# Start-up products, order of sums and the last pairs in a four-layer modulated 1-D convolution kernel

## The chip, the core and the metric

The kernel runs on one core of one Trainium2 chip. The metric is device time in microseconds (us) for one execution, as the median of several runs; the kernel before takes 500.55 us (three runs, 499.84 to 500.64). One more execution was recorded by the profiler. All times inside the kernel are counted from the start of that execution's span.

The engines are TensorE (PE; its weight loads are shown as PEld), VectorE (DVE), ScalarE (ACT), GpSimd (POOL) and SyncE (SP, which issues nearly all DMAs here). SBUF is the working memory, PSUM the memory that PE writes its products to. Each engine runs its own instructions in the order of the program and waits on semaphores for the others. All data are fp32; on PE a product of fp32 operands shows as two passes in the trace, each with its own weight load, so counts of PE rows are twice the number of products in the code.

## The reference

128 samples, each with 64 channels and 1024 positions, go through four convolution layers whose weights are modulated by a style vector per sample, and the input is added at the end:

```python
def _layer(x, style, w, b, mw, mb, typ):
    s = style @ mw.T + mb
    weight = SCALE * w * s[:, None, :, None]
    demod = lax.rsqrt(jnp.sum(weight * weight, axis=(2, 3)) + EPS)
    weight = weight * demod[:, :, None, None]
    if typ == 'same':
        out = jax.vmap(_conv_same)(x, weight) + b[None, :, None]
    elif typ == 'upsample':
        out = jax.vmap(_conv_up)(x, weight.transpose(0, 2, 1, 3)) + b[None, :, None]
        out = _blur(out, 2.0 * blur_k, (1, 1))
    elif typ == 'downsample':
        xb = _blur(x, blur_k, (2, 2))
        out = jax.vmap(_conv_down)(xb, weight) + b[None, :, None]
    return out

out = x
for i, typ in enumerate(('same', 'upsample', 'same', 'downsample')):
    out = _layer(out, style, weights[i], biases[i], mod_w[i], mod_b[i], typ)
return x + out
```

Each layer has 64 input and 64 output channels and three taps. There is no nonlinearity between the layers, so for one sample the whole network, its two blurs included, is one linear filter with nine taps, apart from a few positions at both ends.

## The kernel before

The kernel uses that. For every sample it multiplies the four layers' weights into one nine-tap filter and applies this filter to the sample's input. Samples are held in 64 pairs (two samples fill the 128 partitions); one iteration q of the main loop (L1040, 32 iterations) handles pairs p = 2q and p + 1, and prepares filters and inputs of later ones.

**The filter chain.** For four samples at a time: `scale3` scales the last layer's weights by the table `tA` into `wd`; `stage1` (products L346 into `psS`) joins them with layer 2 and copies the result, scaled by `tB`, to `S`; `stage2` (products L377 into `psR`) joins `S` with layer 1 and the blurs, which are held ready in the nine tiles of `E`, and copies to `R`, scaled by `tC`; `stage3` (products L414 into `psW`, two parts) joins `R` with layer 0 into the filter `Wf`. `combine` (L446, DVE) makes from `Wf` the further filters `H` that a fast form of the convolution needs, with fewer products and more additions.

**The convolution of one pair.** `pre1(p)` makes sums `G` of shifted inputs on DVE (L483, L488), issues the load of a third of a later pair's input, and lets POOL make two of the five rows of `T` (L494, L495). `pre2(p)` makes the other three on DVE (L506, L516) and issues the load of the other two thirds. PE computes three products: `convA12` and, later, `convA3` write `psA`; ACT copies the first of them, negated, to `m` (L561). Then DVE forms the sums: `seed1` makes `u`, `v` and `y`, and `seed2` writes two sums into the PSUM tile `Y`, into which the products of `convB` are then accumulated. (All of these are L567.) [...] `output` (L613 on ACT, L615 on DVE) scales the result and adds the constant, `store` writes it out (L618). `Y` is one tile for nearly all pairs, so `seed2` of the next pair waits until `output` of this one has read it. In the last iterations separate PSUM tiles take its place (`Y2`).

**The order.** The program sets the order by hand; there is no scheduler (`manual_schedule`). `seed` is `seed1` and `seed2`. Ahead of the loop stand the parameter loads, the first products with the style (L189), the sums of squares (`q2_sum`, `var_matmul`, L210), the square root on ACT (`var_root`, L221), reciprocals and Newton steps on DVE, the tables on POOL and DVE, and the filters of the first samples. `blur_scale` (L286) makes four scaled copies `w1s` of layer 1's weights on ACT; `blur_matmul` (L290) sums them, tap by tap, with the identity as the other factor, into two banks of `Y`; `blur_copy` (L309) copies both to `E`. Tables and constants come for 16, then 16, then the remaining 96 samples (`PART`); those of the later parts are spread over the first iterations (`SLOTS`, `EXTRA`). The end positions of all samples are computed by a small side path, for which POOL clears some tiles (`zeros`, L719, 13 memsets; their first reader comes in q=9).

In an iteration the part that matters here is

```python
        convA12(p + 2)
        if q:
            if q < NQ - 2:
                pre2(p + 3)
            store(p, 0)
            if q == 1:
                seed2(p + 1)
            pre1(p + 4)
            store(p, 1)
            if q > 1:
                seed(p + 1)
```

after which come the second part of `stage3`, `convA3(p + 2)` and `convB(p + 1)`, whose accumulation needs `seed2(p + 1)`. SP takes loads and stores in this same order, each waiting for its data.

Of the kernel before, what the change touches and what calls it, by code (L numbers as in the profile page):

```python
# [48 lines left out]
F32 = mybir.dt.float32  # L49
# [5 lines left out]
C = 64  # L55
K = 3
# [7 lines left out]
def kernel(  # L64
# [13 lines left out]
    NQ = B // 4  # L78
# [55 lines left out]

# [3 lines left out]
    nc_v.memset(Z, 0.0)  # L138
# [147 lines left out]
    def blur_scale():  # L286
        for i in range(K + 1):
            nc_a.activation(w1s[:, i], w1r, AF.Copy, scale=BLUR2[i])

    def blur_matmul(ps):  # L290

        for b in range(len(BLUR2)):
            w = w1s[:, min(b, len(BLUR2) - 1 - b)]
            for r, rows in enumerate(HALF):

                both = b % 2 == r
                src = w[rows, 0::2] if both else w[rows, 1]
                at = (b if both else b + 1) // 2
                for cols in HALF:
                    nc.tensor.matmul(  # L300
                        ps[r][cols, C * at : C * (at + 1 + both)],
                        idn[rows],
                        src,
                        start=(b == 0),
                        stop=(b == len(BLUR2) - 1),
                        skip_group_check=True,
                    )
# [58 lines left out]
    def stage2(q, pool=None, engs=(nc_a, nc_a), between=None):  # L366
        st = chain[q]
        ps = unit(pool or ps_w, f"psR{q}")
        for n, e in enumerate((-2, -1, 0, 1, 2, 3, 4, 5, 6)):
            if e % 2 == 0:  # L370
                a, lo, m = slice(0, 5, 2), e // 2 + 1, 3
            else:
                a, lo, m = slice(1, 4, 2), (e + 3) // 2, 2
            for r, rows in enumerate(HALF):
                for c, cols in enumerate(HALF):
                    src = st[c if r == 0 else 1 - c]
                    nc.tensor.matmul(  # L377
                        ps[r][cols, lo * C : (lo + m) * C],
                        E[rows, e // 2 + 1 + (e % 2) * 5, :],
                        src[rows, a, :],  # L380
                        start=(n == 0),
                        stop=(n == 8),
                        skip_group_check=True,
                    )
# [133 lines left out]
    def pre2(p):  # L518
        pre2a(p)
        pre2b(p)  # L520
# [70 lines left out]
    def seed(p):  # L591
        seed1(p)
        seed2(p)

# [280 lines left out]
    L2, L01, L3 = slice(2, 3), slice(0, 2), slice(3, 4)  # L875
    zeros_to_y(2, 512)
# [4 lines left out]
    blur_scale()  # L881
# [8 lines left out]
    var_root(PART[0], pm[0][1], L2)  # L890
    nc_a.activation(wsq[T, L3], wio[T, L3], AF.Square)
# [4 lines left out]
    scale3(0, BOTH)  # L896
    q2_sum(L01)
    blur_copy(psB, BOTH)
# [55 lines left out]
    convA3(1)  # L954
    pre1(2)
    pre2(2)
    const_rest(2, PART[0], const_of(2, PART[0]))
    var_root(PART[1], var_of(PART[1]))
    combine(1)
    seed1(1)  # L960
# [79 lines left out]
    for q in range(NQ):  # L1040
        p = 2 * q
        c, s = q + 2, q + 3
        if q == 1:
            nc.sync.dma_start(Xe, x_ends)
            zeros()
# [19 lines left out]
        convA12(p + 2)  # L1065

        if q:
# [3 lines left out]
            if q == 1:  # L1071
                seed2(p + 1)
            pre1(p + 4)
            store(p, 1)
            if q > 1:
                seed(p + 1)
            if q == NQ - 2:
                pre2(p + 3)
        else:
# [3 lines left out]
            pre2(p + 3)  # L1083
# [3 lines left out]
            for of in (table_C, vector_c0, table_3, vector_Da):  # L1087
                of(PART[1])
            pre1(p + 4)
# [4 lines left out]
        if q == NQ - 2:  # L1094
            convA12(p + 3)
            convA3(p + 3)
        side = SLOTS.get(q)
        convB(p + 1, (lambda: slot(*side)) if side else None)
        if q == NQ - 2:
            seed(p + 2)  # L1100

            Y2[p + 3] = unit(ps_conv, "Y3")
            zeros_to_y(2, 2 * NB, p + 3)
            seed(p + 3)
        output(p + 1, 0)
        output(p + 1, 1, nc_a if q < NQ - 2 else nc_v)
        if c == NQ - 1:
# [94 lines left out]
```

## Time and profile before

| | |
|---|---|
| median of three runs | 500.55 us (499.84 to 500.64) |
| profiled execution | 501.63 us, of which span 499.8 us |
| mean granted PE clock over the span | 0.998 |
| busy: PE / DVE / ACT / POOL | 487.3 / 443.5 / 323.0 / 135.2 us |
| instructions: PE / DVE / ACT / POOL | 12620 / 937 / 787 / 195 |
| `psA` products (convA), 64x170 | 4608 passes, 304 ns each, 208.8 us busy |
| `Y` products (convB), 64x170 | 3072 passes, 304 ns each, 141.9 us busy |
| HBM read / written | 35.46 / 33.62 MB |

Passes on PE overlap (the 64x64 tiles of the array work side by side), so the mean length of one pass is several times the spacing at which they follow one another; spacing is read from the timeline, as the time of a group over its count. DVE's instructions overlap a little too: one begins up to 0.1 us before the last one's end. A time after an instruction in a timeline row, in brackets, is the idle time before it and what ended it.

In the profiled execution the loop begins at about 33 us (products of `stage2(2)`), and from about 120 us on one iteration takes 14.4 us.

### The profile page before, as it was taken

The numbers are of one execution on the slowest core, as the hardware profiler recorded it, in microseconds if no ns is written. First come the engines' busy times: TensorE is split into PE (matmuls) and PEld (weight loads), VectorE is DVE, ScalarE is ACT, GpSimd is POOL, SyncE is SP. The second block draws the span as 40 slices with busy tenths as digits, with TensorE's granted clock in tenths as the row PEclk, the third lists the DMA queues.
The fourth block names the chain that finished last, engine by engine and source line by source line (L and its number), as shares of the span: only waits on it lengthen the run. The fifth ranks groups of instructions, "written<-read, shape, count | busy, mean of one in ns | idle before, by whom it ended". The sixth has DMA issues, their size and how long they took to land.

```text
span 499.8 us, 28326 instructions
## 1 busy us (share of the span) xinstructions
PE 487.3 (97%) x12620; PEld 476.7 (95%) x12620; DVE 443.5 (89%) x937; ACT 323.0 (65%) x787; POOL 135.2 (27%) x195
## 2 busy tenths in 40 slices
PE   7999899999999999999999999999999999999994
PEld 5899889999999999999999999999999999999994
DVE  4989999999999979987979998869999989888895
ACT  3546666677676667666667666667667667766653
POOL 2234533344222222222122122212222212221210
PEclk9999999999999999999999999999999999999999
DMA  8124554454454444443544454444444446443123
GB/s 260 45 90 139 169 155 138 145 169 139 132 163 147 141 144 146 142 155 126 149 145 148 134 157 146 145 134 145 143 145 148 152 128 186 142 148 130 65 109 127
DMA packets 37449, 70.90 MB, mean 142 GB/s; under 512 B 4176, under 2 KB 28752, under 8 KB 37328
## 3 DMA queue, kind: packets, MB, share of 16 engines
q1 hardware_dynamic: 37248, 68.85, 43.8%
q8 instruction: 99, 1.62, 1.4%
q10 hardware_dynamic: 80, 0.25, 0.1%
q14 instruction: 22, 0.18, 0.1%
HBM read 35.46 MB, written 33.62 MB: 138 GB/s over the span
## 4 chain that ended last, share of the span: by engine, by line
PE 84%; DVE 11%; DMA 2%; issue 1%; ACT 1%; SPq 0%; DVEq 0%; ACTq 0%
PE psA L534 28%; PE Y L534 20%; PE psR L377 15%; PE psW L414 12%; PE psS L346 6%; PE psE L763 2%; DVE Y L567 2%; DVE T L516 1%; DVE G L483 1%; DMA par_oi<-in_params_oi 1%; DVE u L567 1%; DVE v L567 1%; DVE G L488 1%; DMA out<-o 1%; DVE T L506 1%
## 5 line engine op out<-in xcount | busy, mean ns | idle before, releaser
L534 PE MATMUL psA<-T,H 64*64 64x170 f32 x4608 | 208.8, 304 | 0.3 <-ACT R L324 0.3
L534 PEld LDWEIGHTS psA<-T,H 64*64 64x64 f32 x4608 | 191.8, 133 | 1.2 <-ACT R L324 0.5
L534 PE MATMUL Y<-T,Wf 64*64 64x170 f32 x3072 | 141.9, 304 | 3.1 <-DVE Y L567 3.1
L494 POOL TENSOR_TENSOR T<-G 128x342 f32<-128x342 f32 x62 | 58.0, 935 | 315.7 <-DVE G L488 187.3
L534 PEld LDWEIGHTS Y<-T,Wf 64*64 64x64 f32 x3072 | 129.5, 133 | 4.7 <-ACT m L561 3.4
L613 ACT ACTIVATE o<-Y,oc,dm 128x340 f32<-128x340 f32 (+1 forms) x126 | 80.0, 635 | 56.1 <-PE Y L534 54.5
L414 PE MATMUL psW<-R,par_oi 64*64 64x256 f32 (+3 forms) x1536 | 101.0, 349 | 0.0
L567 DVE SCALAR_TENSOR_TENSOR Y<-psA,u 128x340 f32<-128x340 f32 (+1 forms) x134 | 66.7, 502 | 36.8 <-ACT o L613 34.1
L377 PE MATMUL psR<-S,E 64*64 64x192 f32 (+1 forms) x2304 | 94.4, 299 | 0.1
L324 ACT ACTIVATE Wf<-psW,t 128x256 f32<-128x256 f32 (+1 forms) x252 | 75.5, 382 | 23.0 <-PE psW L414 22.9
L414 PEld LDWEIGHTS psW<-R,par_oi 64*64 64x64 f32 x1536 | 87.1, 133 | 2.7
L377 PEld LDWEIGHTS psR<-S,E 64*64 64x64 f32 x2304 | 87.4, 133 | 0.3 <-ACT S L324 0.2
L324 ACT ACTIVATE R<-psR,tC 128x448 f32<-128x448 f32 x63 | 36.6, 631 | 54.9 <-PE psR L377 54.9
L613 ACT ACTIVATE o<-y,oc,dm 128x170 f32<-128x170 f32 x125 | 65.7, 526 | 0.0
L495 POOL TENSOR_TENSOR T<-G 128x342 f32<-128x342 f32 x62 | 59.4, 957 | 0.0
L516 DVE TENSOR_TENSOR T<-G 128x684 f32<-128x684 f32 x64 | 57.8, 903 | 0.0
L483 DVE SCALAR_TENSOR_TENSOR G<-X 128x688 f32<-128x688 f32 x64 | 56.3, 879 | 0.0
L346 PE MATMUL psS<-wd,par_oi 64*64 64x192 f32 x768 | 46.2, 329 | 0.0
L346 PEld LDWEIGHTS psS<-wd,par_oi 64*64 64x64 f32 x768 | 38.6, 136 | 0.5 <-ACT raw L631 0.3
L561 ACT ACTIVATE m<-psA 128x340 f32<-128x340 f32 x64 | 29.2, 456 | 12.8 <-PE psA L534 5.3
L567 DVE SCALAR_TENSOR_TENSOR y<-psA,v 128x340 f32<-128x340 f32 x64 | 32.7, 511 | 2.2
L488 DVE SCALAR_TENSOR_TENSOR G<-X 128x342 f32<-128x342 f32 x64 | 33.4, 521 | 0.0
(132 smaller groups left out, 385.2 us busy)
## 6 DMA issues: line engine op xcount, KB each, us to landing
out<-o SPq DMA_DIRECT2D x126, 255.0 KB, 2.9
X<-in_x SPq DMA_DIRECT2D x60, 344.0 KB, 3.1
X<-in_x SPq DMA_DIRECT2D x60, 172.0 KB, 3.2
X<-in_x SPq DMA_DIRECT2D x4, 516.0 KB, 6.7
Xe<-in_x_ends SPq DMA_DIRECT2D x1, 512.0 KB, 4.9
par_oi<-in_params_oi SPq DMA_DIRECT2D x2, 208.0 KB, 5.1
out<-o SPq DMA_DIRECT2D x2, 170.0 KB, 3.3
par_io<-in_params_io ACTq DMA_DIRECT2D x1, 240.0 KB, 4.1
```

The source lines that it names most:

```text
L324: nc_a.activation(dst, src, AF.Copy, scale=f)
L346: nc.tensor.matmul(ps[r][cols, k * C : (k + K) * C], woi[rows, 2, k, :], src[rows, :], start=(k == 0), stop=(k == K - 1), skip_group_check ...
L377: nc.tensor.matmul(ps[r][cols, lo * C : (lo + m) * C], E[rows, e // 2 + 1 + (e % 2) * 5, :], src[rows, a, :], start=(n == 0), stop=(n == 8 ...
L414: nc.tensor.matmul(ps[r][cols, (lo - t_lo) * C : (hi - t_lo) * C], woi[rows, 0, k, :], rt[c][rows, lo - k : hi - k, :], start=(k == order[0]),
L483: nc_v.scalar_tensor_tensor(g[:, PL:], X[:, : 2 * PL], 0.5, X[:, PL:], op0=ALU.mult, op1=ALU.subtract)
L488: nc_v.scalar_tensor_tensor(plane(g, 2), plane(X, 3), 0.5, plane(X, 2), op0=ALU.mult, op1=ALU.subtract)
L494: eng.tensor_add(t[:, 2, :NJ], plane(g, 2), plane(g, 1))
L495: eng.tensor_sub(t[:, 3, :NJ], plane(g, 2), plane(g, 1))
L516: nc_v.tensor_sub(t[:, 0:2, :NJ], both(a, PL), both(b, 1))
L534: nc.tensor.matmul(ps[s][cols], w, Ts[p][rows, SLOT[m], j : j + NB], start=(g == 0 and m not in (0, 4)), stop=(g == 2), skip_group_check=True,
L567: nc_v.scalar_tensor_tensor(out, x, f, y, op0=ALU.mult, op1=ALU.add)
L613: nc_a.activation(dst, src, AF.Identity, bias=add, scale=d3)
```

## The change

Six things are changed.

1. `Z` is cleared in two halves, and `zeros_to_y(2, 256)` is put ahead of the first `zeros_to_y(2, 512)`, `zeros_to_y(2, 192)` ahead of `blur_matmul`.
2. `blur_scale` runs in two parts, with the square root of layer 2 (`var_root`) between them.
3. `blur_matmul` takes each tap offset with all its taps that fall into a bank in one product: bank 0 holds tiles 0 to 4 of `E`, bank 1 tiles 5 to 8, now in rising order of the tap (so `stage2` finds them at another index). 28 products of 64 or 128 columns (56 passes) become 18 of 64 to 192 (36 passes). `blur_copy` has both copies on ACT, ahead of `q2_sum(L01)`.
4. Ahead of the loop `seed1(1)` and `combine(1)` come before `pre2(2)`; in iteration 0 `pre2(3)` comes after the tables of the second part. In iterations 1 and 2 the sums of pair p + 1 come before `pre2(p + 3)` and `pre1(p + 4)`.
5. `zeros()` moves from iteration 1 to iteration 5.
6. In iteration 30 `convA3` of the last pair comes after `convB` of pair 61 and the first half of its output, the second half of the output comes ahead of the last pair's sums, and `seed_last` writes these into PSUM before it makes `v` and `y`.

On DVE this gives, in q=1: `Y` of pair 3, then `pre2(5)`, `pre1(6)`, `pre2(6)`, `pre1(7)`; in q=2: the sums of pair 5, then `pre2(7)`, `pre1(8)`, `pre2(8)`, `pre1(9)`. The order on SP's queue stays, and so does the number of instructions on DVE and POOL but for the second memset of `Z` and the copy that goes to ACT.

```diff
@@ -131,11 +131,11 @@
     one = const.tile([P, 1], F32, name="one")
     eps = const.tile([P, 1], F32, name="eps")
     Z = const.tile([P, 512], F32, name="Z")
-
     E = const.tile([P, NT, C], F32, name="E")
     w1s = const.tile([P, K + 1, K, C], F32, name="w1s")
     nc_v.memset(one, 1.0)
-    nc_v.memset(Z, 0.0)
+    nc_v.memset(Z[:, :256], 0.0)
+    nc_v.memset(Z[:, 256:], 0.0)
     nc_v.memset(eps, EPS)
 
     nc_a.activation(one, one, AF.Sqrt)
@@ -283,26 +283,32 @@
         table(nc_g, t3, bs, ALT, ODD, dm[:, 3, bs], var[:, 3, bs])
 
 
-    def blur_scale():
-        for i in range(K + 1):
+    def blur_scale(ks):
+        for i in ks:
             nc_a.activation(w1s[:, i], w1r, AF.Copy, scale=BLUR2[i])
 
     def blur_matmul(ps):
 
-        for b in range(len(BLUR2)):
-            w = w1s[:, min(b, len(BLUR2) - 1 - b)]
+
+        n = len(BLUR2)
+        plan = [[], []]
+        for b in range(n):
+            for r, (lo, hi) in enumerate(((0, 5), (5, NT))):
+                i, j = max(lo, b), min(hi, b + K)
+                if i < j:
+                    plan[r].append((b, i, j, lo))
+        for k in range(max(map(len, plan))):
             for r, rows in enumerate(HALF):
-
-                both = b % 2 == r
-                src = w[rows, 0::2] if both else w[rows, 1]
-                at = (b if both else b + 1) // 2
+                if k >= len(plan[r]):
+                    continue
+                b, i, j, lo = plan[r][k]
                 for cols in HALF:
                     nc.tensor.matmul(
-                        ps[r][cols, C * at : C * (at + 1 + both)],
+                        ps[r][cols, C * (i - lo) : C * (j - lo)],
                         idn[rows],
-                        src,
-                        start=(b == 0),
-                        stop=(b == len(BLUR2) - 1),
+                        w1s[rows, min(b, n - 1 - b), i - b : j - b],
+                        start=(k == 0),
+                        stop=(k == len(plan[r]) - 1),
                         skip_group_check=True,
                     )
 
@@ -376,7 +382,7 @@
                     src = st[c if r == 0 else 1 - c]
                     nc.tensor.matmul(
                         ps[r][cols, lo * C : (lo + m) * C],
-                        E[rows, e // 2 + 1 + (e % 2) * 5, :],
+                        E[rows, e + 2, :],
                         src[rows, a, :],
                         start=(n == 0),
                         stop=(n == 8),
@@ -592,6 +598,17 @@
         seed1(p)
         seed2(p)
 
+    def seed_last(p):
+
+        m1, m2, m3 = part.pop(p)
+        u, v = m_tile("u", p), m_tile("v", p)
+        y1s[p] = mpool.tile([P, 2, NB], F32, tag="y1", name=f"y1_{p}", bufs=3)
+        sum_of(u, m2, -1.0 / 3.0, m1)
+        part[p] = m3, u
+        seed2(p)
+        sum_of(v, m2, 1.0 / 3.0, m1)
+        sum_of(y1s[p], m3, 2.0 / 6.0, v)
+
     os = {}
 
     def convB(p, between=None):
@@ -873,12 +890,13 @@
     LATER = slice(PART[0].stop, B)
     n_later = NL * (B - PART[0].stop)
     L2, L01, L3 = slice(2, 3), slice(0, 2), slice(3, 4)
+    zeros_to_y(2, 256)
     zeros_to_y(2, 512)
     nc_v.tensor_scalar_mul(mbs, mb, SCALE)
     mod_matmul(PART[0], pm[0][0])
 
     nc_a.activation(wsq[T, L2], wio[T, L2], AF.Square)
-    blur_scale()
+    blur_scale((0, 1))
     zeros_to_y(2, 256)
     mod_scale(PART[0], pm[0][0])
     mod_square(PART[0])
@@ -888,14 +906,16 @@
     var_matmul(PART[0], pm[0][1], (2,))
     nc_v.tensor_mul(wsq[T, L01], wio[T, L01], wio[T, L01])
     var_root(PART[0], pm[0][1], L2)
+    blur_scale((2, 3))
+    zeros_to_y(2, 192)
     nc_a.activation(wsq[T, L3], wio[T, L3], AF.Square)
     psB = [Y[:, r] for r in range(2)]
     blur_matmul(psB)
     first_inverse(PART[0])
     table_A(PART[0], d2)
     scale3(0, BOTH)
+    blur_copy(psB, (nc_a, nc_a))
     q2_sum(L01)
-    blur_copy(psB, BOTH)
     q2_sum(L3)
     table_0(PART[0])
     table_02(PART[0])
@@ -952,12 +972,13 @@
     const_first(2, PART[0])
     var_matmul(PART[1], var_of(PART[1]), start=False)
     convA3(1)
+
     pre1(2)
-    pre2(2)
     const_rest(2, PART[0], const_of(2, PART[0]))
     var_root(PART[1], var_of(PART[1]))
+    seed1(1)
     combine(1)
-    seed1(1)
+    pre2(2)
     pre1(3)
 
 
@@ -1042,6 +1063,7 @@
         c, s = q + 2, q + 3
         if q == 1:
             nc.sync.dma_start(Xe, x_ends)
+        if q == 5:
             zeros()
         if c < NQ:
             stage2(c)
@@ -1063,16 +1085,16 @@
                         store(p + 1, r, slice(0, NB) if i == 0 else slice(NB, HO))
             break
         convA12(p + 2)
-
         if q:
+            if q < 3:
+
+                (seed2 if q == 1 else seed)(p + 1)
             if q < NQ - 2:
                 pre2(p + 3)
             store(p, 0)
-            if q == 1:
-                seed2(p + 1)
             pre1(p + 4)
             store(p, 1)
-            if q > 1:
+            if q > 2:
                 seed(p + 1)
             if q == NQ - 2:
                 pre2(p + 3)
@@ -1080,12 +1102,12 @@
             store(p, 0)
             store(p, 1)
             seed2(p + 1)
-            pre2(p + 3)
             var_inverse(PART[1])
             var_newton(PART[1])
             table_A(PART[1], dm[:, 2, PART[1]])
             for of in (table_C, vector_c0, table_3, vector_Da):
                 of(PART[1])
+            pre2(p + 3)
             pre1(p + 4)
         EXTRA.get((q, 0), lambda: None)()
         if c < NQ:
@@ -1093,17 +1115,18 @@
         convA3(p + 2)
         if q == NQ - 2:
             convA12(p + 3)
-            convA3(p + 3)
         side = SLOTS.get(q)
         convB(p + 1, (lambda: slot(*side)) if side else None)
+        output(p + 1, 0)
         if q == NQ - 2:
             seed(p + 2)
+            convA3(p + 3)
 
             Y2[p + 3] = unit(ps_conv, "Y3")
             zeros_to_y(2, 2 * NB, p + 3)
-            seed(p + 3)
-        output(p + 1, 0)
         output(p + 1, 1, nc_a if q < NQ - 2 else nc_v)
+        if q == NQ - 2:
+            seed_last(p + 3)
         if c == NQ - 1:
 
             banks = unit(ps_w, "Y2")
```

## The prediction

> **What bounds the kernel now.** I read the page first: TensorE (PE) is busy 97% of the span and holds 84% of the chain that ended last, so in the long middle only less PE work or fewer PE gaps could help, and the change takes no PE work out of the middle.
>
> ```profile
> PE 487.3 (97%) x12620; PEld 476.7 (95%) x12620; DVE 443.5 (89%) x937; ACT 323.0 (65%) x787; POOL 135.2 (27%) x195
> ...
> PE 84%; DVE 11%; DMA 2%; issue 1%; ACT 1%; SPq 0%; DVEq 0%; ACTq 0%
> ```
>
> Next the waits of the whole trace: PE stood still three times for the sums that VectorE (DVE) writes into `Y`. The timeline places them at convB(3) (58.82, after 1.47), convB(5) (75.23, after 1.34) and convB(11) (119.81, after 0.27).
>
> ```profile
> PE Y L534 <- DVE Y L567: 3.1, 3, 1.5
> ```
>
> Then the waits of DVE alone from 28 to 121 us: two for ACT's read of `Y` (0.40 at 79.64, 0.98 at 88.90) and one at 28.41 for `m`. Otherwise its instructions touch.
>
> ```profile
> DVE Y L567 <- ACT o L613: 1.4, 2, 1.0
> DVE u L567 <- ACT m L561: 0.9, 1, 0.9
> ```
>
> The stretches say the same: DVE is full from 41 to 75 and nearly so to 120, and eases only later (12.41 of 14.40).
>
> ```profile
> core 0: us, PE busy (x) PEld busy (x) DVE busy (x) ACT busy (x) POOL busy (x), PEclk, DMA share, GB/s
> 57.00:75.00 18.00, 15.42 (x398) 14.62 (x390) 17.72 (x35) 11.06 (x29) 10.19 (x21) 1.00 0.67 201
> 105.00:120.00 15.00, 14.73 (x393) 14.30 (x389) 14.70 (x31) 10.57 (x27) 6.73 (x11) 1.00 0.52 147
> 300.00:314.40 14.40, 14.40 (x392) 14.40 (x388) 12.41 (x26) 9.89 (x24) 3.59 (x4) 1.00 0.50 148
> ```
>
> So: from about 28 to 120 DVE sets the pace, afterwards PE. Last the start, PE only:
>
> ```profile
> 1.48 1.98 PE L170 MATMUL Y<-Z 64*64 64x512 f32 x8 [1.48 <-DVE eps L139]
> 4.89 1.13 PE L170 MATMUL Y<-Z 64*64 64x256 f32 x8
> 6.82 0.69 PE L300 MATMUL Y<-w1s,par_oi 64*64 64x128 f32 x4 [0.48 <-ACT w1s L288]
> 7.81 2.29 PE L300 MATMUL Y<-w1s,par_oi 64*64 64x64 f32 x50 [0.30 <-DMA par_oi<-in_params_oi]
> ...
> 10.00 2.13 PE L346 MATMUL psS<-wd,par_oi 64*64 64x192 f32 x22
> ```
>
> and the tile `psS` in the first 25 us, where the same 64x192 product takes 524 ns early and 322 late:
>
> ```profile
> L346 PE MATMUL psS<-wd,par_oi x72: 322/323/524, 9.8 to 21.0; 64*64 64x192 f32 x72
> ```
>
> PE runs at about half pace at first: 24 passes of `psS` cost 2.1 us at 10.0 and 0.97 at 60.9. Weight loads fall from 228 ns to 133 at 13.1 us, though the clock column prints 1.00 throughout. The fast pace came 5.3 us after the last gap of PE (0.30 before 7.81); earlier gaps are 0.46 at 3.46 and 0.48 at 6.34.
>
> **The change, part by part. (1) Start.** The halved memset of `Z` (0.48) lets PE begin 0.24 sooner, at about 1.25. One more fill of 256 columns (8 passes, 1.13 measured for such a group, some 0.9 where groups overlap) closes the gap up to 3.92; it may push the `par_s` products by up to 0.3, which `q` (ready 5.88) mostly hides. The fill of 192 columns (about 0.7) closes 6.34 to 6.82. The first four blur passes then last until the second `par_oi` half lands (7.76). PE has no gap left from 1.25 on, unless the 16-column products (3.92 to 4.96) count as one. If 5.3 us without a gap are enough, PE is fast by 1.25 + 5.3 = 6.6; if the count starts behind the 16-column products, by 10.2; if the fills count for nothing, at about 13 as before.
> The square root L221 moves ahead of two of the four `w1s` scalings (0.28 each): 6.86 to about 6.4, so `wd` is ready at 8.5 in place of 8.98. That hides under the blur products and is worth nothing while they end later.
> Blur: 56 passes become 36 with the same 5376 columns. Only four (768 columns) can precede 7.81. The remaining 4608 columns cost, at the slow 0.45 ns per column (2.1 us / 24 / 192), about 2.05: end 9.85, against 10.1. At the fast 0.21 (0.97 us) they cost 0.97, or 1.12 at 35 ns per pass (72 `psR` passes in 2.50): end 8.95. `blur_copy` moves its second half (0.42) from DVE to ACT, which idles 1.35 there; DVE had waited for ACT's half anyway, so no cost.
> Stage 1 follows (2.1 slow, 0.97 fast), then ACT's `S` (before: 12.04). `R` (15.77) needs `tC`, which DVE and POOL finished at 15.52, 3.5 after `S`. So `R` comes at `S` + 3.5 where PE is fast. Fast by 6.6: `S` 10.05, `R` 13.6, gain 2.15. Fast by 10.2: `S` 11.1, `R` 14.6, gain 1.2. Slow: gain 0.35. From `R` to `u` at 28.41 the same chain follows, and DVE has 0.94 of waiting there, so the gain is carried whole. I take 2.15, because the 5.3 is an upper bound on what PE needed; 0.35 stays in the range.
> [...]
>
> **(2) Before and in iteration 0.** `pre2(2)` leaves its place behind `pre1(2)`. Before, its L516 cost 1.58 in place of 0.86, since POOL added `T` then; L700 behind it cost 0.69. Now DVE reaches `var` early, but `var` waits for ACT's `nw`, which stands behind `m` (33.48 to 33.93) and ends 34.3. `seed1(1)` and `combine(1)` queue behind that wait. Line by line (`u`, `v`, `y` 1.38, `combine` 2.85, `pre2` 1.21, `pre1` 1.20) the sums of pair 1 end at 42.05 against 41.77, just before convB(1) at 42.19. Then `pre2(3)`, moved behind the PART[1] tables, escapes its own collision (1.58), and `u` of pair 2 comes at 46.6 against 46.67: zero, bounds -0.1 to +0.45. The loads issued with `pre2` and `pre1` move with them, and stores behind them on SP by at most one seed (2.4); their data is used some 29 us later.
>
> **(3) Iterations 1 and 2: sums first.** In q=1 `Y` of pair 3 begins at 55.7 rather than 57.62 and ends 56.7, before PE arrives (57.08): convB(3) gains 1.7. In q=2 the whole seed (2.36) goes ahead of `pre2(7)` and `pre1(8)`, and convB(5) loses its wait too. But DVE does no less work. And POOL's two `T` additions, released by `pre1`, used to run beside sums from PSUM; now they run beside `pre2` and the next `pre1`. What that costs stands in q=1 of before, DVE first, POOL second:
>
> ```profile
> 60.22 0.87 DVE L516 TENSOR_TENSOR T<-G 128x684 f32<-128x684 f32 x1
> 61.00 1.59 DVE L483 SCALAR_TENSOR_TENSOR G<-X 128x688 f32<-128x688 f32 x1
> 62.51 1.22 DVE L488 SCALAR_TENSOR_TENSOR G<-X 128x342 f32<-128x342 f32 x1
> ```
> ```profile
> 60.31 1.55 POOL L494 TENSOR_TENSOR T<-G 128x342 f32<-128x342 f32 x1
> 61.81 1.54 POOL L495 TENSOR_TENSOR T<-G 128x342 f32<-128x342 f32 x1
> ```
>
> They take turns: 59.79 to 63.65 took 3.86, the same four at 84.04 to 86.45 took 2.41. For q=2 that puts 3.86 where 2.78 stood (74.99 to 77.77): +1.1. POOL's `T` of pair 9 slides behind the POOL tables (2.76) into `combine(4)`: one more collision of 0.73 is likely (0 to 1.2). Against it DVE loses its two waits, 0.40 and 0.98. Sum at `Y` of pair 7: 1.1 - 0.40 + 0.73 - 0.98 = +0.45, so convB(7) is released 0.45 later than before and PE's gain of q=1 and 2 is given back there. From there DVE's instructions touch up to convB(11) (119.81), so 0.45 stays; bounds -0.7 and +1.5.
> [...]
>
> **(4) Rest.** `zeros()` (13 memsets, 58.40 to 60.37) goes to q=5, where POOL idles from 114.0 to 117.4 and DVE's operations beside memsets kept their length: 0 (if DVE did feel it, 0.3). In the last iterations PE's work is only reordered; before, PE was short of work by 0.17 once (seeds of pair 63, 491.6). Now `m` of pair 63 waits for convA3(63) and ACT's output, about 490.1; `u` and `Y` take 1.5 and end 491.65, PE arrives 491.75: -0.1, bounds -0.3 and +0.4. The tail of outputs and stores after 493.6 stays.
>
> **Sum:** -2.15 + 0 + 0.45 + 0 - 0.1 = -1.8. The profiled execution took 501.63 with a span of 499.8, 1.83 lying around it; it would become 499.83, span 498.0. The runs' median is 1.08 below that execution, so 500.55 - 1.8 = 498.75.
>
> **Rivals.** *Start stays slow or turns late*: fills of zeros or 16-column products may not bring the fast pace forward. For: the fill before 3.46 brought none. Against: gaps followed it. Gain 0.35 to 1.2, net 0 to -0.85: about 500.1.
> *DVE's debt decides (slower)*: from 28 to 120 DVE has 1.38 of waits to give; if `combine(4)` meets both additions (1.2) and q=0 costs 0.45, the sum is +1.4, and with a start of 0.35 the time is 501.6. It decides once the loop loses 1.0 more than the start gains. For: DVE full at 119.81. Against: the start.
> *Both waits are won*: PE keeps 1.75 + 1.62. Against: convB(11) waited already, and its release can come sooner only by DVE's 1.38. With a fast start and no collision: 500.55 - 2.15 - 1.38 = 497.0.
>
> **How the numbers follow.** Forecast 0.46, slow or late start 0.27, DVE's debt 0.19, waits won 0.08. Within 0.2% (1.0 us) is what this kernel's runs cannot tell from no change. Nine tenths of the forecast are faster (0.41), a fifth of the second (0.05), all of the last (0.08): 0.54. Slower: 0.17 of the third. The rest, 0.29, is the same. Range 497.5 to 501.3: it cuts half of either end case. The forecast's own range is 498.0 to 499.7.
>
> **What would show it.** Right: weight loads near 133 ns in the blur or in stage 1, `S` at about 10 to 11, `u` of pair 0 at 26.2; no wait at convB(3) and convB(5), but one of about 1 at convB(4) or convB(7); L483 or L516 near 1.6 in q=2; PE without gaps from 120 less 1.7. Wrong: `S` after 11.5; DVE waiting in q=3 to 5, which would mean more slack than I count; a wait at convB(63).

## The result and the profile after

The changed kernel takes 500.55 us as the median of 14 runs (499.13 to 501.15); the kernel before, run beside it, takes 500.51 (14 runs, 499.64 to 501.08). The ratio is 0.9998 with a 95% interval of 0.9989 to 1.0007: no difference that can be measured. The time lies in the stated range (497.5 to 501.3), but the forecast of 498.75 did not come. Of the cases named, the first rival (about 500.1) lies nearest, though not for its reason alone.

The profiled execution of after took 501.05 us with a span of 499.24. Before's took 501.63 (span 499.85), which is above every one of its 14 runs. So the two traces differ by 0.6 where the medians do not differ at all. Of that, 0.50 lies behind the last scaling of an output, in the last stores: this tail took 4.21 in before, 3.71 in after, and 3.64 to 4.11 in the eight traces below, with either order of the end. What the change does is therefore read at landmarks inside the trace:

| us from the span's start | before | after | after less before |
|---|---|---|---|
| `S` of the first samples | 12.04 | 11.54 | -0.50 |
| `R` | 15.77 | 15.03 | -0.74 |
| `u` of pair 0 | 28.41 | 27.73 | -0.68 |
| `stage2` (its first weight load) in iterations 2 and 3 | 64.20, 81.16 | 61.78, 77.84 | -2.42, -3.32 |
| `stage2` in iteration 4 | 95.68 | 94.58 | -1.10 |
| `stage2` in iteration 29 (about the same from 6 on) | 465.89 | 465.12 | -0.77 |
| last product of PE | 493.57 | 493.46 | -0.11 |

The start gained 0.7, the early loop gained 2.6 more and gave all of it back, and the last iterations lost 0.65. The page shows the same shares as before, busy times and chain:

```profile
PE 487.2 (98%) x12616; PEld 474.9 (95%) x12616; DVE 444.0 (89%) x937; ACT 322.5 (65%) x788; POOL 133.7 (27%) x195
...
PE 85%; DVE 11%; issue 1%; ACT 1%; DMA 1%; SPq 0%; DVEq 0%
```

The waits of the whole trace, after (who waits, for whom; total, times, longest). PE's waits for the sums in `Y` had been 3.1 us in three pieces:

```profile
PE Y L540 <- DVE Y L573: 2.8, 3, 1.7
```

Still three, and nearly as much. The timeline of PE says which (start, duration, and in brackets the idle time before):

```profile
65.25 1.96 PE L540 MATMUL Y<-T,Wf 64*64 64x170 f32 x48 [0.53 <-DVE Y L573]
...
89.30 1.10 PE L540 MATMUL Y<-T,Wf 64*64 64x170 f32 x24 [1.72 <-DVE Y L573]
```

```profile
491.50 1.96 PE L540 MATMUL Y<-T,Wf 64*64 64x170 f32 x48 [0.52 <-DVE Y L573]
```

The waits at convB(3) and convB(5) (1.47 and 1.34 before) are gone. In their place stand convB(4) at 65.25, convB(7) at 89.30 and, in the last iterations, convB(63) at 491.50. The waits of DVE between 24 and 121 us show what it had to give and gave, its two waits for ACT's read of `Y` (1.4):

```profile
DVE u L573 <- ACT m L567: 0.9, 1, 0.9
DVE var L222 <- ACT nw L221: 0.6, 1, 0.6
```

And the stretches, where DVE is as full as before and PE's gap has only moved, from 57 to 75 (15.42 busy before, 17.26 now) into 75 to 90:

```profile
core 0: us, PE busy (x) PEld busy (x) DVE busy (x) ACT busy (x) POOL busy (x), PEclk, DMA share, GB/s
...
57.00:75.00 18.00, 17.26 (x453) 15.99 (x450) 17.76 (x34) 10.86 (x28) 4.70 (x6) 1.00 0.56 172
75.00:90.00 15.00, 13.28 (x348) 12.52 (x344) 14.79 (x29) 9.95 (x25) 8.61 (x13) 1.00 0.60 182
```

**The start.** PE's timeline of after:

```profile
1.22 2.84 PE L170 MATMUL Y<-Z 64*64 64x256 f32 x16 [1.22 <-DVE Z L137]
3.98 0.81 PE L189 MATMUL psM<-par_s 128*64 128x16 f32 x16
4.72 0.66 PE L170 MATMUL Y<-Z 64*64 64x256 f32 x8
5.78 0.23 PE L210 MATMUL psM<-ssq,q 64*64 64x16 f32 x2 [0.39 <-DVE q L205]
...
7.57 2.04 PE L306 MATMUL Y<-w1s,par_oi 64*64 64x64 f32 x32 [0.49 <-DMA par_oi<-in_params_oi]
9.33 2.11 PE L352 MATMUL psS<-wd,par_oi 64*64 64x192 f32 x24
```

The rows `Y<-Z` are the fills: products with the zero tile `Z` that `zeros_to_y` issues into `Y`. The eight passes at 4.72 take 0.66 where the same group took 1.13 in before: PE does turn fast early, sooner than the 6.6 us I forecast. But a fill that takes 0.66 in place of 1.13 ends sooner, and what it was to cover comes open again, 0.39 ahead of 5.78 and 0.49 ahead of 7.57. And the blur (32 passes in 2.04) and `stage1` (24 passes in 2.11, the slow figure of before) run at the slow pace again. Stretches of after, with the granted clock in the third column from the right:

```profile
core 0: us, PE busy (x) PEld busy (x) DVE busy (x) ACT busy (x) POOL busy (x), PEclk, DMA share, GB/s
...
4.40:7.80 3.40, 2.42 (x44) 1.29 (x46) 2.49 (x13) 1.96 (x8) 0.80 (x4) 1.00 1.02 281
7.80:11.20 3.40, 3.40 (x56) 3.24 (x49) 1.41 (x5) 1.14 (x3) 2.73 (x10) 0.50 1.02 410
11.20:13.10 1.90, 1.52 (x43) 1.39 (x41) 1.31 (x4) 1.56 (x5) 0.00 (x0) 1.00 0.28 98
```

The clock falls to 0.50 from 7.80 to 11.20, behind 3.40 us in which PE was busy for only 2.42. Blur and `stage1`, which were to gain, fall into just this stretch.

This is one execution. The clock averaged over the span is on record for all 14 runs (0.993 to 1.000), and a stretch of 3.4 at 0.50 would take 0.003 off it, so the ten runs at 0.998 and above held no such stretch. Their median is 500.54 (499.13 to 500.96). The slow stretch alone therefore cannot be why the forecast did not come. How early the pace turned in those runs is not known, since the average does not show the slow pace ahead of the first turn (before's column prints 1.00 there too).

**The turns of DVE and POOL** fall where the prediction had them. After, q=2, DVE first, POOL second:

```profile
75.29 1.59 DVE L489 SCALAR_TENSOR_TENSOR G<-X 128x688 f32<-128x688 f32 x1
76.81 1.22 DVE L494 SCALAR_TENSOR_TENSOR G<-X 128x342 f32<-128x342 f32 x1
...
80.30 1.12 DVE L458 SCALAR_TENSOR_TENSOR H<-Wf 128x384 f32<-128x384 f32 x1
```

```profile
74.67 1.48 POOL L500 TENSOR_TENSOR T<-G 128x342 f32<-128x342 f32 x1 [9.92 <-PE Y L540]
76.10 1.55 POOL L501 TENSOR_TENSOR T<-G 128x342 f32<-128x342 f32 x1
...
80.07 0.94 POOL L501 TENSOR_TENSOR T<-G 128x342 f32<-128x342 f32 x1
```

L489 takes 1.59 (0.87 alone) and L494 1.22 (0.50 alone) beside POOL's two additions, and the first operation of `combine(4)` 1.12 (0.55 alone) beside the addition at 80.07. That they take turns by whole instructions is seen in the ends: POOL 76.15, DVE 76.88, POOL 77.65, DVE 78.03. Each ends 0.73 to 0.77 behind the other engine's end, the shorter L494 0.38 behind it.

### The profile page after: what moved, and what is told of

Same layout as the page of the kernel before. It is cut to its first block, busy times and chain, and to the rows that moved or that the text cites. A ratio compares the mean times of both kernels' runs of the same rounds, so it can differ in the third digit from the quotient of the medians.

```text
span 499.2 us, 28320 instructions
## 1 busy us (share of the span) xinstructions
PE 487.2 (98%) x12616; PEld 474.9 (95%) x12616; DVE 444.0 (89%) x937; ACT 322.5 (65%) x788; POOL 133.7 (27%) x195
## 4 chain that ended last, share of the span: by engine, by line
PE 85%; DVE 11%; issue 1%; ACT 1%; DMA 1%; SPq 0%; DVEq 0%
PE psA L540 29%; PE Y L540 19%; PE psR L383 15%; PE psW L420 13%; PE psS L352 6%; PE psE L780 2%; DVE T L522 2%; DVE G L489 2%; DVE Y L573 2%; DMA par_oi<-in_params_oi 1%; DVE G L494 1%; DVE u L573 1%; DVE T L512 1%; DVE v L573 1%; DVE H L458 0%
## 5 line engine op out<-in xcount | busy, mean ns | idle before, releaser
L500 POOL TENSOR_TENSOR T<-G 128x342 f32<-128x342 f32 x62 | 57.6, 929 | 318.5 <-DVE G L494 189.7
L501 POOL TENSOR_TENSOR T<-G 128x342 f32<-128x342 f32 x62 | 58.6, 946 | 0.0
L522 DVE TENSOR_TENSOR T<-G 128x684 f32<-128x684 f32 x64 | 57.0, 890 | 0.0
L489 DVE SCALAR_TENSOR_TENSOR G<-X 128x688 f32<-128x688 f32 x64 | 56.9, 889 | 0.0
L494 DVE SCALAR_TENSOR_TENSOR G<-X 128x342 f32<-128x342 f32 x64 | 33.2, 519 | 0.0
```

What stands on the lines that cost most here:

```text
L489: nc_v.scalar_tensor_tensor(g[:, PL:], X[:, : 2 * PL], 0.5, X[:, PL:], op0=ALU.mult, op1=ALU.subtract)
L494: nc_v.scalar_tensor_tensor(plane(g, 2), plane(X, 3), 0.5, plane(X, 2), op0=ALU.mult, op1=ALU.subtract)
L500: eng.tensor_add(t[:, 2, :NJ], plane(g, 2), plane(g, 1))
L501: eng.tensor_sub(t[:, 3, :NJ], plane(g, 2), plane(g, 1))
L522: nc_v.tensor_sub(t[:, 0:2, :NJ], both(a, PL), both(b, 1))
```

## The experiments

Three runs take the change apart, three test a cause each, one changes the writes at the end, and one puts the answers together. The theory of the start that they test is a guess from after's clock, which stood at 0.50 for 3.4 us behind 3.40 us with only 2.42 busy: that the pace is set in stretches of this length, which may begin elsewhere in another execution, that a busy stretch brings the fast pace and that one with gaps brings the slow pace back. The theory of the loop is DVE's debt and its turns with POOL (1.59 for 0.87 above). A ratio is taken over all runs and is not quite that of the two medians. "Net" below is always the time between two landmarks of a trace, so that a run's own start or tail does not enter. Of each trace, `u` of pair 0 to `stage2` of iteration 6 is called the loop (96.67 us in before, 96.60 in after), and `stage2` of iteration 29 to PE's last product the end (27.68 and 28.34).

**The start alone** (items 1 to 3 of the change in the kernel before).

```diff
-    nc_v.memset(Z, 0.0)
+    nc_v.memset(Z[:, :256], 0.0)
+    nc_v.memset(Z[:, 256:], 0.0)
...
+    zeros_to_y(2, 256)
     zeros_to_y(2, 512)
...
-    blur_scale()
+    blur_scale((0, 1))
...
     var_root(PART[0], pm[0][1], L2)
+    blur_scale((2, 3))
+    zeros_to_y(2, 192)
```

> Only the start-up edits (fills, halved clear of Z, square root sooner, larger blur products, both copies on ACT) on the kernel before. Theory A (PE's pace is granted by stretches of time of which a busy one releases the slow pace and one with gaps brings it back): the first sums of pair 0 (u, 28.41 before, 27.73 after the whole change) come anywhere from 25.8 to 28.4 according to the run, with slow weight loads (near 228 ns) somewhere between 6 and 12 us in most of them; the median stays within 0.15% of before. Theory B (the fast pace is owed a fixed time after the first product, so the start gains a fixed amount): u at 27.7 again, and a median 0.7 us (0.14%) lower. Both: waits at convB(3) and convB(5) of about 1.5 us as before, since the loop's order is as before.

Measured: 500.89 against 501.46, ratio 0.9992 (0.9983 to 1.0002). Here PE's timeline shows another start than after's, with the same code:

```profile
4.34 1.04 PE L190 MATMUL psM<-par_s 128*64 128x16 f32 x16 [0.28 <-DMA par_s<-in_params_s]
5.31 1.13 PE L171 MATMUL Y<-Z 64*64 64x256 f32 x8
...
7.26 2.46 PE L307 MATMUL Y<-w1s,par_oi 64*64 64x192 f32 x36
9.53 1.17 PE L353 MATMUL psS<-wd,par_oi 64*64 64x192 f32 x24
```

The fill at 5.31 is slow (1.13), the blur too, and only `stage1` is fast (1.17). `S` comes at 10.81, `R` at 14.29 and `u` at 26.94, 1.47 ahead of before: the "fast by 10.2" case of the prediction. The same start code gives `u` between 27.60 and 27.87 in after and in four runs below. Before's own start varies as much: `u` at 28.41, 27.39 and 28.69 in the three traces that have it. The means are 27.60 (six traces) and 28.16 (three), so the start is worth some 0.6 by the traces, and 0.57 by the medians of this run. Neither is clear of the spread: starts of the same code lie 0.9 to 1.3 apart, and the interval of the ratio takes in 1.

**The loop alone** (items 4 and 5).

```diff
+        if q == 5:
             zeros()
...
+            if q < 3:
+                (seed2 if q == 1 else seed)(p + 1)
             if q < NQ - 2:
                 pre2(p + 3)
...
-            if q > 1:
+            if q > 2:
                 seed(p + 1)
```

> Only the order of sums ahead of and in iterations 0 to 2, and the later clearing, on the kernel before. Theory DVE's debt (DVE sets the pace to about 120 us; waits of PE are moved, not removed): from u of pair 0 to convB(11) 91.3 to 91.5 us as in both kernels (91.40 before, 91.32 after); no wait at convB(3) and convB(5), about 0.5 at convB(4) and 1.7 at convB(7); median within 0.1% of before. Theory PE's waits (each wait that is removed is time won): 88.0 to 88.5 us from u to convB(11), median 3 us (0.6%) lower.

Measured: 501.30, ratio 0.9993 (0.9983 to 1.0002); the loop 96.54, so -0.13 net. `stage2` comes 2.46 and 3.12 earlier in iterations 2 and 3 (this trace's start is 1.02 early), 1.53 earlier in iteration 4, and PE waits 1.36 at convB(7). The gain of the two waits is won and given back with no help from the start or the end. In iterations 23 to 27 this trace loses another 0.5 against before, in two steps that after does not show; their cause was not found.

**The end alone** (item 6).

```diff
             convA12(p + 3)
-            convA3(p + 3)
...
+        output(p + 1, 0)
         if q == NQ - 2:
             seed(p + 2)
+            convA3(p + 3)
...
-            seed(p + 3)
-        output(p + 1, 0)
         output(p + 1, 1, nc_a if q < NQ - 2 else nc_v)
+        if q == NQ - 2:
+            seed_last(p + 3)
```

> Only the reordered last pairs on the kernel before. Theory late seeds: the four writes of the last pair's sums into Y follow one another at 0.38 us and take 1.48, so convB(63) waits 0.5 us where it waited 0.15, and PE ends 0.4 to 0.65 us later relative to convB(11) (373.8 from convB(11) to PE's end before, 374.4 after); the stores after PE's end are done 0.5 sooner (4.2 us from the last scaling to the end before, 3.7 after); sum 0.0 to 0.2 us. Rival (the last stores were what the edit was for, and they carry the end): span 0.5 us shorter from convB(11) to the end.

Measured: 501.94, ratio 1.0008 (0.9999 to 1.0016). The loop is before's to the hundredth (96.67) and the end takes 28.35, 0.67 more, with the same wait of 0.52 at convB(63). So the end's order costs what after loses there. The tail behind the last scaling took 3.95, not the 0.5 less than before's 4.21 that was expected; before's order itself gave 3.80, 4.11 and 3.64 in other traces, so the tail does not hang on this order.

**More fill ahead of the blur** (in after; the fills only hold PE busy).

```diff
     blur_scale((0, 1))
-    zeros_to_y(2, 256)
+    zeros_to_y(2, 512)
...
     blur_scale((2, 3))
-    zeros_to_y(2, 192)
+    zeros_to_y(2, 512)
+    zeros_to_y(2, 512)
```

> The changed kernel with fills that keep PE busy at the fast pace as well: 512 columns in place of 256 behind the style products, twice 512 in place of 192 ahead of the blur. Theory A (gaps bring the slow pace back): weight loads of the blur and of stage 1 near 133 ns, S near 10 to 10.8, R near 13.6 to 14.2, u of pair 0 at 26.2 to 27 and a median 0.6 to 1.5 us below the changed kernel's. Theory B (a fixed time): the pace turns at 11 to 13 us whatever the fill, the blur starts later behind the fills (8.5 to 9.5) and the median is 1 to 2 us above.

Measured: 502.07 against 501.46, ratio 1.0008 (0.9992 to 1.0023). PE was without a gap from 1.22 on and yet slow until about 9 (four weight loads took 0.38 at 8.49 and 0.21 at 9.26); the fills ended at 9.9 and held the blur up, so `S` came at 12.32. So the pace, once fast, stayed so through the start (clock 1.00 up to 20), as the theory of stretches has it, but the time expected from it is missed, since the fills themselves were in the way. And one part of the theory fails: counted back in steps of 3.413 from the slow stretch that begins at about 91.0 (below), which is an estimate, the stretch from about 2.3 to 5.7 was busy throughout, and the slow pace went on for another 3.4. In it stand the 16 products of 16 columns, 1.04 long, which pass no more than 256 columns. What this run shows beyond the question is at convB(7), in stretches around its wait of 2.00 (until 90.03):

```profile
85.00:91.00 6.00, 4.00 (x113) 3.65 (x104) 5.93 (x13) 3.17 (x10) 2.77 (x5) 1.00 0.58 175
91.00:94.50 3.50, 3.50 (x56) 3.50 (x54) 3.29 (x6) 1.66 (x5) 1.41 (x2) 0.51 0.39 113
94.50:100.00 5.50, 5.50 (x161) 5.50 (x157) 5.21 (x15) 2.60 (x8) 0.38 (x1) 1.00 0.41 130
```

A wait of 2.00 was followed by a slow stretch (0.51 over 3.50) of the same length as in after's start (0.50 over 3.40), and the loop took 97.74, 1.14 more than after's.

**POOL's two rows of `T` on DVE for pairs 6 and 8** (in after).

```diff
-            pre1(p + 4)
+            pre1(p + 4, nc_v if q < 3 else nc_g)
```

> The changed kernel, but in iterations 1 and 2 DVE makes the two rows of T of pairs 6 and 8 itself (two additions of 0.43 us each) in place of POOL. The change's order of sums stays. Theory turns (DVE and POOL take turns on SBUF operands, and DVE's debt is what holds PE up to 120 us): the additions cost DVE 0.86 per pair, the two collisions per pair that they replace cost 1.44 and 1.43, and POOL's T of pair 9 no longer reaches combine(4) (0.57); L489 and L522 are back at 0.87 everywhere in q=1 and 2, and from u of pair 0 to the first product of stage 2 in iteration 6 it takes 94.9 us (96.60 in the changed kernel, 96.67 before). Rival (POOL's additions cost DVE nothing that PE feels; more work on DVE is more debt): 98.3 us.

Measured: 500.33 against 501.13, ratio 0.9983 (0.9972 to 0.9994). DVE in q=2:

```profile
73.34 0.51 DVE L494 SCALAR_TENSOR_TENSOR G<-X 128x342 f32<-128x342 f32 x1
73.89 0.52 DVE L500 TENSOR_TENSOR T<-G 128x342 f32<-128x342 f32 x1
74.32 0.51 DVE L501 TENSOR_TENSOR T<-G 128x342 f32<-128x342 f32 x1
...
75.95 0.87 DVE L489 SCALAR_TENSOR_TENSOR G<-X 128x688 f32<-128x688 f32 x1
```

DVE does two instructions more and every operation around them keeps its short length. In q=1 one collision stays (1.59 at 56.20; in after 1.59 at 56.17), beside the additions for pair 5. The wait at convB(7) falls from 1.72 to 0.20, and the loop takes 95.24, 1.36 less. So the turns with POOL, those of q=1 that before has too among them, cost about half of the 2.6 that was given back. The other half is still given back here, as DVE's debt would have it.

**`pre1` of pair 8 ahead of the sums in q=2** (in after; POOL's additions then run beside sums out of PSUM).

```diff
-            if q < 3:
-                (seed2 if q == 1 else seed)(p + 1)
+            if q == 1:
+                seed2(p + 1)
+            if q == 2:
+                pre1(p + 4)
+                seed(p + 1)
...
-            pre1(p + 4)
+            if q != 2:
+                pre1(p + 4)
```

> The changed kernel, but in iteration 2 the order is pre1(8), the sums of pair 5, pre2(7): POOL's additions for pair 8 run beside sums from PSUM again, and the sums still come 1.2 us sooner than before the change. Theory turns and debt: no collision in q=2 (1.43 and 0.57 saved), 94.6 us from u of pair 0 to stage 2 of iteration 6 (96.60 in the changed kernel); convB(7) waits 0 to 0.3 where it waited 1.72. Rival (PE is held by something else than DVE at convB(7)): within 0.2 of 96.60.

Measured: 500.35, ratio 0.9987 (0.9977 to 0.9997); the loop 95.43, 1.17 less than after's. The wait at convB(7) is gone, and one at convB(5) is back, on the timeline of PE:

```profile
73.45 1.10 PE L540 MATMUL Y<-T,Wf 64*64 64x170 f32 x24 [1.07 <-DVE Y L573]
```

The loop falls 0.8 short of the 94.6 expected, and this wait is the likely reason: the sums of pair 5 now stand behind 1.2 us of `pre1`.

**Two writes for the last pair's sums in place of four** (in after: both banks in one tile, so that `seed2` writes each of its two sums whole).

```diff
+        elif p == NP - 1:
+            banks = [(slice(0, 2), whole[0])]
...
-            Y2[p + 3] = unit(ps_conv, "Y3")
+            whole.append(ps_conv.tile([P, 2, 512], F32, tag="u", name="Y3"))
+            Y2[p + 3] = [whole[0][:, r, :] for r in range(2)]
```

> The changed kernel, but the last pair's sums go into their PSUM tile in two writes over both banks in place of four of one bank each. Theory late seeds (the four writes wait for one another): the writes take 1.06 us in place of 1.48, convB(63) waits 0.1 in place of 0.52, and from the first product of stage 2 in iteration 29 to PE's end it takes 27.9 us (28.34 in the changed kernel, 27.68 before). Rival (u comes too late, behind the output that was moved ahead): 28.3.

Measured: 500.82 against 501.13, ratio 1.0000 (0.9989 to 1.0010); the end takes 27.95, 0.39 less than after's and 0.27 more than before's. First the rows of after for pairs 62 and 63, then those of this run (DVE for pair 63, and PE's last products):

```profile
486.46 1.06 DVE L573 SCALAR_TENSOR_TENSOR Y<-psA,u 128x170 f32<-128x170 f32 x4
...
489.97 1.48 DVE L573 SCALAR_TENSOR_TENSOR Y<-psA,u 128x170 f32<-128x170 f32 x4
```

```profile
490.04 1.08 DVE L574 SCALAR_TENSOR_TENSOR Y<-psA,u 128x340 f32<-128x340 f32 x2
```

```profile
489.10 4.03 PE L541 MATMUL Y<-T,Wf 64*64 64x170 f32 x96
```

The writes shrink by 0.40 and PE no longer stands still; but 96 products that took 3.76 in before's order still take 4.03, so they arrive a little late all the same. The median cannot resolve 0.4. Four writes are not slow as such: pair 62's four, of the same shape, took 1.06. They go into two tiles (`unit` makes two from `ps_w` and one from `ps_conv`) and start 0.24 apart, each begun before the last has ended. Pair 63's go into one tile, and each begins 0.03 behind the end of the one before it, 0.38 from start to start.

**All together**: after's start; `pre1` first in q=2; `T` of pair 6 on DVE; before's order of the end with two writes.

```diff
+            if q == 2:
+                pre1(p + 4)
+                seed(p + 1)
...
-                pre1(p + 4)
+            if q != 2:
+                pre1(p + 4, nc_v if q == 1 else nc_g)
...
             convA12(p + 3)
+            convA3(p + 3)
...
+            seed(p + 3)
+        output(p + 1, 0)
         output(p + 1, 1, nc_a if q < NQ - 2 else nc_v)
-        if q == NQ - 2:
-            seed_last(p + 3)
```

> The change's start; q=1 as in the change but with T of pair 6 made on DVE; q=2 with pre1(8), sums of pair 5, pre2(7); the end in the order of before with the last pair's sums in two writes. If debt, turns and late seeds are right: 94.0 to 94.3 us from u of pair 0 to stage 2 of iteration 6 (96.67 before), 27.5 from stage 2 of iteration 29 to PE's end (27.68 before), so 2.4 to 2.8 us less than before at an equal start, plus up to 1 us from the start; median ratio to before 0.993 to 0.996. Rival (the pace of PE early in the run outweighs all of this): ratio within 0.999 to 1.001.

Measured: 499.26 against 501.13, ratio 0.9959 (0.9947 to 0.9972). It is faster than before by 1.4 to 2.7 us; after was not run beside it, but has before's median. The loop takes 94.78 (-1.89), the end 27.60 (-0.08 against before, which is no more than noise: the same order as before's took 27.85 in the trace of the loop alone). The waits of the whole trace no longer hold one of PE for the sums in `Y`; what is left of PE in `Y` behind the start is 0.2 for ACT's copy of `Wf` and

```profile
PE Y L541 <- issue: 0.5, 1, 0.5
```

Added up from the traces, the start's 0.56, the loop's 1.89 and the end's 0.08 make 2.5; the medians show 1.9, and the runs with `T` on DVE and with `pre1` first also fall about 0.5 short of their sums, by their ratios. Each of these lies within its interval (this one's is 1.4 to 2.7 us), and whether the difference is real stays open.

## Why the prediction was right in its range and wrong in its sum

The range held the time because it was wide enough to hold no change at all; the sum behind it failed. That sum was -2.15 + 0 + 0.45 + 0 - 0.1 = -1.8. The traces give, in the same order, -0.68 for the start, -0.08 for everything up to iteration 6, and +0.65 at the end: -0.1, and with the mean start of the nine traces, -0.56, nothing. The medians show nothing. Two terms failed, by 1.6 and by 0.75; that of the sums was 0.5 too high, and the three together make the miss of 1.8.

**The start, -2.15, is the first step that failed.** The step read "PE has no gap left from 1.25 on", with the fills priced at the slow pace they had in before (1.13 for 256 columns, 0.7 for 192). Its first half was right, for PE was fast by 4.4. But then the fills took 0.66 and 0.62, the gaps they were to close opened again, and from 7.80 to 11.20 the clock fell to 0.50, just where the gain should have come (0.97 us each for blur and `stage1`; measured 2.04 and 2.11). I treated the fast pace as something that, once there, stays, and as something that a PE without gaps is sure to bring. More fill showed that the second fails too: where the fast pace came late, the exception that I had named and then set aside, that the products of 16 columns count as a gap, is the one that fits (fast at about 9 there; `stage1` fast, 1.17, from 9.53 in the start alone and from 10.19 in the combined run; I had 10.2 for this case). The run of the start alone shows the other outcome of the same code, fast late and for good, with a gain of 1.47; no trace reached `u` at 26.2. For the ten runs of after without a slow stretch no trace was kept, so what their start lost can only be argued from these. The rest of the step held: `R` came 3.49 behind `S` (I said 3.5), and from `R` to `u` 12.70 passed as against 12.64, so the gain was carried whole. No run shows that 5.3 us without a gap bring the fast pace, on which the -2.15 stood: after was fast 3.2 behind its first product (1.22 to 4.385), the run with more fill only some 8 behind it, without a gap between. What the runs showed in its place is a clock that changes 3.413 apart (4.385, 7.798 and 11.211 in after), at another place in another execution: with one and the same start code the fill of 256 columns took 0.66 in after and 1.13 in the start alone. Busy time alone did not bring the fast pace: with more fill the slow one went on behind a stretch of 3.4 without a gap. The last section has a count for these stretches.

**Iteration 0, at 0, was a little low:** relative to the shift of the start, `u` of pair 2 came 0.26 sooner, outside the bounds of -0.1 and +0.45.

**The sums first, +0.45: the mechanism right, the sizes a little off.** As forecast, convB(3) and convB(5) no longer wait, the debt of DVE comes due at convB(4) and convB(7), and there all is given back. Against the shift of the start, `u` of pair 6 is 0.86 late, which is 1.12 from `u` of pair 2 on (the collisions of q=2, charged 1.1), the operation in `combine(4)` costs 0.57 more (charged 0.73), the wait of 0.40 vanished, which leaves DVE 0.94 late at the end of `combine(4)`, and with the wait of 0.98 gone too, `Y` of pair 7 is 0.13 early where I had it 0.45 late. Moving `T` off POOL (1.36 gained) and `pre1` ahead of the sums (1.17) show that the turns cost about half of what was given back. That an operation of `combine` is held up by the additions at all, on which the 0.73 stood, no row of before showed; in after the first one of `combine(4)` took 1.12 for 0.55 beside POOL.

**`zeros()` at 0 held:** the shift is -0.83 in iteration 5, where it now stands, and -0.76 behind it.

**The end, -0.1, is the second step that failed,** and it is a term mis-sized: "`u` and `Y` take 1.5". Less the 0.76 that the trace is ahead, `m` of pair 63 ended at 490.02 (I said 490.1) and PE arrived at 491.74 (491.75). But from the start of `u` to the last write of `Y` took 2.09, not 1.5. The last pair's `Y` is written in four halves into one tile, one behind the end of the other (0.38 apart); before's row for them stood at 1.48, and I took 1.06 from the pairs that write it in two. So the sums ended at 492.21 on that clock, and the wait of 0.52 at convB(63), named as a sign against me, is there. Two writes take out 0.39 of the 0.65; the order of before with two writes takes out all of it.

**The rivals.** "Start stays slow or turns late" lies nearest to the time, but in part by luck: in after's trace the fast pace came at 4.385 and was lost again from 7.80 to 11.20 (clock 0.50), in that of `T` on DVE it was lost there too (0.51), and without the end's loss a start worth 0.56 would have given a gain. Of "DVE's debt decides" the debt was right and its price was not: the loop lost nothing net, where +1.4 was charged. "Both waits are won" did not happen, because convB(7) waits once PE arrives early; the combined run has neither wait nor most of the collisions, and took 499.26, not the 497.0 named there.

**The level.** The median lies 1.12 below the profiled execution for before (I took 1.08), but only 0.50 for after, whose profiled execution is one of at most four in 14 with a slow stretch. The sum was made on an execution above all 14 runs, and its first term, the start, varies by 0.9 to 1.3 between executions.

## What to carry to other kernels

A wait won on one engine is kept only if the engine that set it has time to give: sum that engine's own waits up to the place where its instructions cease to touch, and look at what runs beside it, for here about half of the 2.6 us given back hung on which operations met POOL's additions. Filler that is to hold an engine at speed must be sized at the speed it brings: the fill priced at 1.13 took 0.66, and gaps of 0.39 and 0.49 came open behind it. In the stretches counted below, the work that was passed went with the pace and the idle time did not. And a start that hangs on this is a spread of outcomes (0.9 to 1.3 us here), not one number. Price a group of writes by a row with the same count, shape and destination: four writes of half the size took 1.48 into one tile and 1.06 into two.

## What the runs showed of the hardware

- The pace of PE changed at times 3.413 us apart. In after the granted clock rises at 4.385, falls to 0.50 at 7.798 and is back at 1.00 from 11.211; with more fill it averages 0.51 from 91.00 to 94.50 and 1.00 on both sides, a slow stretch of the same length. The place of the changes differs from one execution to the next: before's clock first rises at 13.105, and one and the same start code had its fill of 256 columns fast in after (0.66 at 4.72) and slow in the start alone (1.13 at 5.31).
- Idle time did not go with the pace. In after, PE was busy for 2.43 of the stretch 4.385 to 7.798 and the slow pace followed; it was busy for only 1.69 of 86.305 to 89.718, which holds the wait of 1.72, and none followed. With more fill (stretches counted back from 91.0, an estimate) the slow pace followed a stretch with some 1.4 busy, from about 87.6, with the wait of 2.00, and it went on behind the busy one from about 2.3. The number of columns passed did go with it: a pass of 64x192 counts as 192, spread evenly over its recorded time. After's two stretches passed 5016 (slow next) and 6683 (fast next); the two with more fill some 5400 each (slow next), an estimate from the rows of PE. Over all stretches in the traces of before and after, those with up to 5016 columns were followed by the slow pace and those with 6065 or more by the fast one, whichever pace they ran at themselves. This is a count made afterwards; no run was made to test it, and none of these stretches passed between 5400 and 6065.
- DVE and POOL took turns by whole instructions where POOL's additions for `T` met DVE's operations from `X`, `G` and `Wf`, all of them in SBUF: 1.59 for 0.87 (L489), 1.59 for 0.86 (L522), 1.22 for 0.50 (L494), 1.12 for 0.55 (the first of `combine(4)`). Here it was quicker to let DVE do POOL's two additions (0.51 each, and some 0.7 saved at a collision: 0.87 against 1.59) than to share them. DVE's sums with `psA` in PSUM among their inputs kept their 0.50 to 0.52 beside POOL. Which property of the operands decides, no run was made to show.
